# Exchanging rotary halves by DMA for half of layer 0's query heads

## The chip, the cores and the metric

The kernel runs on one core of one Trainium2 chip. The core has a matrix engine (PE; its weight loads are listed apart as PEld), a vector engine (DVE), a scalar engine (ACT), a general engine (POOL), and a queue engine (SP) that here issues the kernel's DMA transfers. The metric is the device time of one execution in microseconds (us), the median of several runs; less is better. A profile is one further execution with a record of each instruction.

## The reference

The program is a decoder of two layers over 64 sequences of 64 tokens, width 256. Each layer does self-attention, cross-attention to a context of the same shape, and a feed-forward part, each behind a layer norm and added to `x`. The change touches layer 0's self-attention only, of which this part matters:

```python
H, HKV, D = (16, 4, 128)
def _rotate_half(x):
    x1, x2 = jnp.split(x, 2, axis=-1)
    return jnp.concatenate([-x2, x1], axis=-1)
qkv = jnp.einsum('bsh,oh->bso', x, w_qkv)
...
q = _layernorm(q, qn_g, qn_b)
k = _layernorm(k, kn_g, kn_b)
cos, sin = _rope_tables(s, D, ROPE_BASE)
q = q * cos + _rotate_half(q) * sin
k = k * cos + _rotate_half(k) * sin
...
scores = jnp.einsum('bhqd,bhkd->bhqk', q, k) / jnp.sqrt(jnp.float32(D))
```

There are 16 query heads of 128 and 4 key and value heads. The rotation adds to each head, times a cosine, the same head with its two halves of 64 exchanged, times a signed sine.

## The kernel before

The 4096 tokens are worked in 16 groups of 256. A group first goes through layer 0 (sections a0, x0 and f0: self-attention, cross-attention, feed-forward), is stored to `mid`, and later goes through layer 1 (a1, x1, f1). Several groups are in work at once, and the preparation of layer 1's weights is mixed into the groups of layer 0.

The order of the work is written by a planner in the kernel itself, before anything runs. Each helper records operations with `s.o(engine, cost, reads, writes, function)`; `s.alt` records an operation that may go to one of several engines. `Sched.plan` then places all operations in one list, by the costs given and by a due time for each one (`LEAD`, `FINE`, `PACE`, `SHIFT`, with penalties such as `PEN` for using DVE for work that may go elsewhere, and `HOLD` for changing how PE is tiled). Each engine gets its instructions in that fixed order, and so does the queue of SP: an instruction that waits holds up all that is listed behind it on its engine. Tiles come from pools with fixed numbers of buffers: `k2` is 2 KB a partition with 67 buffers, `B` is one PSUM bank, with 8.

In self-attention (`l0_attn`) a group is done in two blocks of eight query heads. For each block, `proj2` makes a bank of keys (`k_ps`, two heads by 256 tokens) and four banks of queries (`q_ps`, two heads each, numbered `c2` = 0 to 3), head elements along the partitions. Weights are centred beforehand, so a norm needs only the sum of squares and a factor, which is applied later. `rope_bank` takes such a bank out of PSUM:

- L832, ACT: two copies of 64 partitions each put the halves, exchanged, into the SBUF tile `sw`.
- L833, ACT: the square of `sw` into `sq`, which PE sums up over partitions into `ss` (L857 for keys, L881 for queries).
- L834, DVE: the bank times the cosines `rp0c` (queries) or `rp4c` (keys) into `qu` or `ku`.
- L835, POOL: `sw` times the sines `rp0s` or `rp4s`.
- L837, POOL or DVE: `sw` is added to `qu` or `ku`.

The sums `ss` then pass a chain: ACT (`sss`, L887), a transpose on PE (`ss_t`, L892), a reciprocal root on DVE (`nr_t`, `nr_y`, L606 to L614), then a factor for the keys (`rb`, `rk`, `kf`, L899 to L911). Scores `s_ps` (L933) need `kf` and the four `qu`. After them come the softmax (`sm_mx`, `sm_sm`, `phl`, L625 to L655), a transpose of `phl` by DMA (L578), the product with the values (`po`, L689), its eviction by ACT (L694) and DVE (L696), and the output projection (`acc`). The values lie in `vt` and are also copied, half a tile of 64 partitions each time, to `vx` and back within `vt` (L668 to L670, from SBUF to SBUF, issued by SP).

Cross-attention of layer 0 has scores `xs_ps` (L1033) whose maxima DVE takes (`xmx`, L1040), collected by `mx_ps`, and scores `xt_ps` (L1067) whose exponentials ACT takes (`xpt`, L1074), multiplied with values into `xo_ps` (L1083) and copied to `so` on ACT or DVE. In layer 1 the banks `qk_ps` become `k8` and `q8` on ACT (two halves) or DVE (L1646, L1650).

Of the kernel before, what the change touches and what calls it, by code (L numbers as in the profile page):

```python
# [9 lines left out]
F32 = mybir.dt.float32  # L10
# [10 lines left out]
S = 64  # L21
# [15 lines left out]
HOLD = 965  # L37
# [698 lines left out]
def l0_attn_setup(e, I):  # L736
# [62 lines left out]
    for i, f in ((0, 128.0 ** -0.5), (4, 1.0)):  # L799
        tb = [s.fixed(c.tile([128, S], F32, name=f"rp{i}{n}")) for n in "csb"]  # L800
        tmp = s.T("k1", [128, S], name="rp_tmp")

        def g(rt, cols, cg, sg, bt, b2, i=i, f=f):
            nc.vector.tensor_scalar(cg, rt[:, 0], cols[:, i:i + 1], f, ALU.mult, ALU.mult)
            nc.vector.tensor_scalar(sg, rt[:, 1], cols[:, i + 1:i + 2], f, ALU.mult, ALU.mult)
            nc.vector.tensor_scalar(bt, rt[:, 0], cols[:, i + 2:i + 3], f, ALU.mult, ALU.mult)
            nc.vector.tensor_scalar(b2, rt[:, 1], cols[:, i + 3:i + 4], f, ALU.mult, ALU.mult)
            nc.vector.tensor_tensor(bt, bt, b2, ALU.add)
        s.o("DVE", 700, [rt, cols], tb + [tmp], g)
        w.tab.append(tb)  # L810
    one = c.tile([128, 3, 32], F32, name="onehot")
# [9 lines left out]
def rope_bank(e, ps, tab, dst):  # L821
# [16 lines left out]
    return sq  # L838


def l0_attn(e, xt):
# [5 lines left out]
    for blk in range(2):  # L847
# [24 lines left out]
        for c2 in range(4):  # L872
            ps = s.T("B", [128, 2, GT], name="q_ps")
            proj2(e, w.u[1 + blk], 256 * c2, xT, ps)
            sqs.append(rope_bank(e, ps, w.tab[0], (qu[c2], lambda t: t)))
# [969 lines left out]
def ctx_scale(e, I, nt):  # L1845
# [16 lines left out]
PEN = 247.38  # L1862
NQ = 1
LEAD = {
    ".xt": -7500, "a0.acc": 6500, "a0.bias_ps": -16000, "a0.bm": -112500, "a0.k_ps": -6000, "a0.kf": -4000,
    "a0.ku": -27000, "a0.ln_mv": 86500, "a0.ln_nb": -120000, "a0.ln_rs": 43000, "a0.ln_st": 60500, "a0.nr_v": -2500,
    "a0.nr_y": -92000, "a0.ohl": -35000, "a0.phl": -9500, "a0.po": -500, "a0.pt": 36500, "a0.qu": -2500,
    "a0.rb": 21500, "a0.rk": 2000, "a0.s1": -4500, "a0.s_ps": -27500, "a0.sm_mx": 120000, "a0.sm_sm": -2500,
    "a0.sq": -2000, "a0.ss": 15500, "a0.ss_t": -7000, "a0.sss": 30500, "a0.sw": 38000, "a0.v_ps": -50000,
    "a0.vt": 84000, "a0.vx": 111500, "a0.xT": -26500, "a0.xh": 112500, "a0.xhl": -29000, "a0.xt": -3000,  # L1870
    "a1.ctx1": -38500, "a1.k1": -120000, "a1.k1_ps": -24500, "a1.ksh": 26000, "a1.kst": -32000, "a1.ln_mv": 96000,
    "a1.ln_nb": -55000, "a1.ln_rs": 68500, "a1.ln_st": 120000, "a1.o1_ps": 47500, "a1.oT1": 23000, "a1.pT": -31000,
    "a1.phl": -101000, "a1.q1": 119500, "a1.q1_d": -9500, "a1.q1_ps": -56500, "a1.q1hl": 26500, "a1.q1st": 120000,
    "a1.s1": 120000, "a1.s1_ps": -90500, "a1.sm_f": -3000, "a1.sm_mx": -76000, "a1.sm_sm": 104000, "a1.v1": 90000,
    "a1.vbd": 10500, "a1.xT": 37000, "a1.xh": -8500, "a1.xhl": -6000, "a1.xt": 73500, "f0.-": -112500,
    "f0.f0_ps": -19500, "f0.f0o_ps": -14500, "f0.hT": -69000, "f0.hm": -120000, "f0.hm_ps": 20500, "f0.ln_mv": -4000,
    "f0.ln_nb": 39000, "f0.ln_rs": 42000, "f0.ln_st": 52000, "f0.xT": 78000, "f0.xh": 24000, "f0.xhl": -18000,
    "f0.xt": -11000, "f1.f1ah": 114500, "f1.f1am": -13000, "f1.f1ix": -115500, "f1.f1o": -116500, "f1.f1o_ps": -4500,
    "f1.f1s2": 73500, "f1.f1sx": 81500, "f1.gu": 8500, "f1.gu_ps": -112500, "f1.hq": -53500, "f1.hqT": 93500,
    "f1.ln_mv": 81500, "f1.ln_nb": -116500, "f1.ln_rs": -3000, "f1.ln_st": 31000, "f1.sig": 32000, "f1.xh": -10500,  # L1880
    "f1.xq": -119500, "f1.xqT": 111000, "f1.xt": 30500, "setup.-": 15500, "setup.a1am": 100500, "setup.am_ps": -4000,
    "setup.bo_ps": 70500, "setup.bo_w": -46500, "setup.cen": -72500, "setup.ctx_a": 64000, "setup.ctxa1": 99000,
    "setup.f_t": -94500, "setup.f_w": 23000, "setup.fam": -23500, "setup.fw_ps": 40000, "setup.g_G": -68500,
    "setup.g_ps": -75500, "setup.g_w": -21000, "setup.l0cols": 87500, "setup.l0ek": 7500, "setup.l0eq": -32500,
    "setup.l0w0": -3500, "setup.l0w1": -120000, "setup.l0w2": 67000, "setup.l0w3": 14000, "setup.l0w4": 96000,
    "setup.n_am1": 11500, "setup.n_o": -60000, "setup.n_ps": -116500, "setup.n_v": 120000, "setup.n_w": -28500,
    "setup.nf": 31500, "setup.p2_ar": -85500, "setup.p2_p2": -64500, "setup.rope_t": -34000, "setup.rp_tmp": -49000,
    "setup.sqj": -80000, "setup.w_a1": -25000, "setup.w_a1o": -110500, "setup.w_am1": -59000, "setup.w_f0": -77500,
    "setup.w_hl": -18500, "setup.w_l0kv": 7000, "setup.w_l0o0": -4000, "setup.w_l0o1": -7500, "setup.w_l0q0": -77000,
    "setup.w_l0q1": 26000, "setup.w_n": 47000, "setup.w_x1ki0": -30500, "setup.w_x1ki1": -15500,  # L1890
    "setup.w_x1q0": -64500, "setup.w_x1q1": 14500, "setup.x1wki0": 18500, "setup.x1wki1": 116500,
    "setup.x1wn0": 33500, "setup.x1wn1": 41000, "setup.x1wn2": 77500, "setup.x1wn3": 56000, "setup.x1wq0": 25500,
    "setup.x1wq1": -93500, "setup.xtwo": -62500, "x0.-": -120000, "x0.cT": -11500, "x0.ctx": 9000, "x0.hl": -82000,
    "x0.hl_d": -42500, "x0.ln_mv": -10000, "x0.ln_nb": -71000, "x0.ln_rs": -118000, "x0.ln_st": -103000,
    "x0.mneg": -99500, "x0.mx_ps": -37500, "x0.so": -80000, "x0.xh": 24500, "x0.xmx": -105500, "x0.xo_ps": 3500,
    "x0.xot_ps": 49500, "x0.xpt": 13500, "x0.xrc": -17500, "x0.xs_ps": -16500, "x0.xt": -41000, "x0.xt_ps": 2500,
    "x0.y": -35000, "x0.yo": -82500, "x1.acc": -38000, "x1.cTs": -120000, "x1.chl": 68500, "x1.ctx": -50000,
    "x1.gac": 42000, "x1.gjk": -34000, "x1.gy_ps": 48000, "x1.k8": -29500, "x1.ln_mv": 74500, "x1.ln_nb": -119500,
    "x1.ln_rs": -55000, "x1.ln_st": 87000, "x1.ms": -111500, "x1.phl": 6000, "x1.pt": 64000, "x1.q8": -90000,
    "x1.qk_ps": 17500, "x1.rkL": 103000, "x1.rkb": -88500, "x1.rkb_ps": -49000, "x1.rms": 24500, "x1.s1": 120000,  # L1900
    "x1.s_ps": -120000, "x1.sm_mx": -22000, "x1.sm_sm": -68500, "x1.vn": 117000, "x1.vn_ps": 68000,
    "x1.x1esc": -45000, "x1.xT": 88000, "x1.xh": 116000, "x1.xhl": 117000, "x1.xt": 23500,
}
RESV = 1e+15
TMIN = {"setup.w_a1": 1457, "setup.w_l0kv": -4579, "setup.w_x1q1": 1916, "setup.x1wki1": -18878, "setup.x1wn0": 1785, "setup.x1wn2": -1297, "setup.x1wn3": -2931, "setup.x1wq1": -2255}
FINE = dict(a=[
    (0, 1, -19000), (1, 1, -500), (2, 1, -9000), (3, 1, -13000), (4, 1, 42000), (5, 1, 22500), (6, 1, -11000),
    (7, 1, 10000), (8, 1, 15500), (9, 1, -39000), (10, 1, 1500), (11, 1, -9500), (12, 1, -12500), (13, 1, -15500),
    (14, 1, -5000), (15, 1, 13000), (16, 1, 4000), (17, 1, 9000), (18, 1, -30500), (19, 1, 21500), (20, 1, -45000),
    (21, 3, 500), (24, 1, -34000), (25, 1, 14000), (26, 1, 30500), (27, 1, 5000), (28, 1, 5500), (29, 1, -9000),  # L1910
    (30, 1, 12500), (31, 1, 7500), (32, 1, 21500), (33, 1, 23500), (34, 1, -2000), (35, 1, 44500), (36, 1, -5000),
    (37, 1, 9000), (38, 1, 10500), (39, 1, 6500), (40, 1, 24000), (41, 1, 10000), (42, 1, 6500), (43, 1, 49000),
    (44, 1, -7000), (45, 1, 9500), (46, 1, 10000), (47, 1, 3000), (48, 1, 15500), (49, 1, 10000), (50, 1, 17000),
    (51, 1, -9500), (52, 1, 9000), (53, 1, 10000), (54, 1, 10500), (55, 1, 35500), (56, 1, 3500), (57, 1, 21000),
    (58, 1, 2500), (59, 1, 4000), (60, 1, -500), (61, 1, 1500), (62, 1, -44500), (63, 1, 2000), (64, 1, 21500),
    (65, 1, -37000), (66, 1, -49500), (67, 1, -14000), (68, 1, -5500), (69, 1, -7500), (70, 1, 1000),
    (71, 1, -12500), (72, 1, 38000), (73, 1, -1000), (74, 1, 500), (75, 1, -5000), (76, 1, 4500), (77, 1, 1000),
    (78, 1, 9000), (79, 1, 2500), (80, 1, -4500), (81, 1, 5000), (82, 1, -17000), (83, 1, -12500), (84, 1, 41500),
    (85, 1, -7000), (86, 1, 3500), (87, 1, 7500), (88, 1, 22000), (89, 1, 20000), (90, 1, -8500), (91, 1, -12500),
    (92, 1, -75000), (93, 1, -9000), (94, 1, -12000), (95, 1, -1000), (96, 1, 8000), (97, 1, -5000),  # L1920
    (98, 1, -3000), (99, 1, 4000), (100, 1, -2500), (101, 1, -3000), (102, 1, 12000), (103, 1, 13500),
# [266 lines left out]
```

## Time and profile before

| | us |
|---|---|
| median of 3 runs | 2370.53 |
| lowest and highest | 2370.43, 2375.34 |
| profiled execution, own time | 2375.9 |
| its span, first to last instruction | 2374.1 |

| engine | busy us | share of the span |
|---|---|---|
| PE | 2168.2 | 91% |
| DVE | 1828.7 | 77% |
| POOL | 1691.1 | 71% |
| ACT | 1594.2 | 67% |

The mean clock granted to PE is 0.962 of full speed. DMA moved 220.82 MB. A share of the whole span is a mean over stages: the stores to `mid` end layer 0's groups between 322.1 and 1438.2 us, and the loads of `mid` begin layer 1's between 1154.7 and 2129.2 us, so that a stage with one limit has to be looked at by itself. In the lists below, an idle time in front of an instruction is put down to what ended it; PE is modelled as pipelined, and some of its records are missing.

### The profile page before, as it was taken

What the parts mean: (1) busy time and instruction counts of PE and PEld (TensorE: products, weight loads), DVE (VectorE), ACT (ScalarE), POOL (GpSimd) and SP (SyncE); (2) the same over time, 40 slices, a digit from 0 to 9 for tenths busy, and PEclk for the clock granted to TensorE, in tenths of its full rate; (3) what the DMA queues carried; (4) which work ended last, traced back from release to release, by engine and by line L of the source; (5) the groups of instructions that cost most, each with busy time, mean ns of one, the idle gap of its engine ahead of it and who ended that gap; (6) DMA issues with size and microseconds to landing.
All of it is one profiled execution on the core that took longest, in us unless ns stands there. A gap on an engine that the chain in (4) does not pass through costs nothing. (4 is left out here: it accounts for less than half of the span.)

```text
span 2374.1 us, 69674 instructions
## 1 busy us (share of the span) xinstructions
PE 2168.2 (91%) x28232; PEld 1692.0 (71%) x28232; DVE 1828.7 (77%) x4256; ACT 1594.2 (67%) x3047; POOL 1691.1 (71%) x1793
## 2 busy tenths in 40 slices
PE   6887889988898978999988999999999999999996
PEld 5765556655565645666645788898888988889885
DVE  7577689877878778788887766778877777777766
ACT  7864878777677768788767675666566655656552
POOL 6897898776857677688945664677777667667642
PEclk9997999999899999999989999999999999999997
DMA  7744444342344234244353353444434444343322
GB/s 233 231 118 104 113 110 115 99 110 64 99 112 95 60 62 90 47 114 104 75 157 77 73 108 66 78 86 77 77 79 78 74 81 83 77 79 77 64 33 41
DMA packets 484322, 220.82 MB, mean 93 GB/s; under 512 B 340568, under 2 KB 463384, under 8 KB 484000
## 3 DMA queue, kind: packets, MB, share of 16 engines
q1 hardware_dynamic: 484000, 216.37, 40.1%
q8 instruction: 222, 3.64, 0.6%
q14 instruction: 100, 0.82, 0.1%
HBM read 89.06 MB, written 34.64 MB: 52 GB/s over the span
## 5 line engine op out<-in xcount | busy, mean ns | idle before, releaser
L1541 PE MATMUL vn_ps<-x1wn,cTs 128*64 128x256 f16 x6144 | 357.9, 273 | 0.5 <-ACT q L1282 0.5
L1074 ACT ACTIVATE xpt<-xt_ps,xes 128x512 f32<-128x512 f32 x512 | 316.2, 699 | 61.8 <-PE xt_ps L1067 56.1
L1541 PEld LDWEIGHTS <-cTs 128*64 128x64 f16 x6144 | 327.1, 110 | 17.0 <-issue 15.1
L1040 DVE TENSOR_REDUCE xmx<-xs_ps 128x2 f32<-128x512 f32 x512 | 316.5, 679 | 27.5 <-PE xs_ps L1033 27.0
L626 POOL TENSOR_TENSOR s<-s,sm_mx 128x1024 f32<-128x1024 f32 x96 | 183.6, 1913 | 196.1 <-DVE sm_mx L625 118.3
L1546 ACT ACTIVATE vn<-vn_ps 128x512 f16<-128x512 f32 x256 | 149.2, 593 | 137.8 <-PE vn_ps L1541 136.2
L1548 DVE SCALAR_TENSOR_TENSOR vn<-vn_ps,vn 128x512 f16<-128x512 f32 x256 | 170.7, 680 | 87.2 <-ACT vn L1546 86.7
L655 POOL TENSOR_TENSOR phl<-s,phl 128x512 f16<-128x512 f32 x192 | 221.9, 1166 | 17.7 <-ACT phl L654 13.4
L652 POOL TENSOR_TENSOR s<-s,sm_sm 128x512 f32<-128x512 f32 x192 | 201.5, 1062 | 7.2
L835 POOL TENSOR_TENSOR sw<-sw,rp0s 128x512 f32<-128x512 f32 x128 | 164.8, 1296 | 15.1 <-ACT sq L833 12.9
L654 ACT CAST phl<-s 128x512 f16<-128x512 f32 x192 | 118.4, 620 | 81.5 <-POOL s L652 80.9
L832 ACT COPY sw<-q_ps 64x512 f32<-64x512 f32 x256 | 146.9, 579 | 32.0 <-PE q_ps L432 24.4
L837 POOL TENSOR_TENSOR qu<-qu,sw 128x512 f32<-128x512 f32 x128 | 163.4, 1283 | 2.0
L1650 ACT ACTIVATE k<-qk_ps,x1kb 128x256 f32<-128x256 f32 x240 | 100.6, 471 | 95.1 <-PE qk_ps L432 94.8
L1083 PE MATMUL xo_ps<-xpt,xve 128*32 128x256 f32 x2048 | 150.6, 404 | 7.9 <-ACT xpt L1074 6.1
L569 ACT ACTIVATE xh<-xt,ln_nb,ln_rs 128x256 f32<-128x256 f32 x192 | 107.2, 599 | 61.2 <-POOL ln_nb L566 60.8
L430 PE MATMUL q_ps<-xT,l0w 128*128 128x256 f16 x512 | 140.8, 275 | 2.0 <-ACT mneg L1044 0.8
L430 PE MATMUL acc<-l0w,ohl 128*128 128x256 f16 x512 | 141.2, 276 | 0.5 <-DVE ohl L696 0.4
L432 PE MATMUL q_ps<-xT,l0w 128*128 128x256 f16 x512 | 140.4, 274 | 0.7 <-DVE l0w L541 0.7
L431 PE MATMUL acc<-l0w,ohl 128*128 128x256 f16 x512 | 141.0, 275 | 0.0
L432 PE MATMUL acc<-l0w,ohl 128*128 128x256 f16 x512 | 140.9, 275 | 0.1
L430 PE MATMUL qk_ps<-cTs,x1wki 128*128 128x256 f16 x512 | 140.8, 275 | 0.0
(416 smaller groups left out, 6697.8 us busy)
## 6 DMA issues: line engine op xcount, KB each, us to landing
ovl<-hl_d SPq DMA_DIRECT2D x96, 128.0 KB
vx<-vt SPq DMA_DIRECT2D x64, 128.0 KB
ctx<-in_ctx_dram SPq DMA_DIRECT2D x32, 256.0 KB
hl_d<-hl SPq DMA_DIRECT2D x64, 128.0 KB
wd<-w_hl SPq DMA_DIRECT2D x32, 256.0 KB
q1st<-q_d SPq DMA_DIRECT2D x128, 64.0 KB
xt<-in_x_dram SPq DMA_DIRECT2D x16, 256.0 KB
ctx_a<-in_ctx_dram SPq DMA_DIRECT2D x8, 512.0 KB
```

Of the source, the lines that this page charges most:

```text
L430: nc.tensor.matmul(out, lh, rh, start=(st and i == 0), stop=False, **kw)
L432: nc.tensor.matmul(out, ll, rh, start=False, stop=(i == n - 1), **kw)
L626: s.o("POOL", 1900, [mx], [s1], lambda m, t: nc.gpsimd.tensor_tensor(t, t, bc(m, 2, 64), ALU.subtract))
L652: s.o("POOL", 1030, [sm], [s1.sub(j)], lambda m, t, h=h: nc.gpsimd.tensor_tensor(t[:, h], t[:, h], bc(m[:, h], 2, 64), ALU.mult))
L655: s.alt([("POOL", c_pool(482), lambda t, _, p, h=h: nc.gpsimd.tensor_tensor(pl(p, 1), t[:, h], pl(p, 0), ALU.subtract)), ("DVE", c_dves(51 ...
L835: s.o("POOL", 1225, [sg], [sw], lambda t, w: nc.gpsimd.tensor_tensor(v(w), v(w), bc(t, 1, 8), ALU.mult))
L837: ("POOL", 1225, lambda w, d: nc.gpsimd.tensor_tensor(view(d), view(d), w, ALU.add))], [sw], [dt])
L1040: nc.vector.tensor_reduce(m[:, h, bs % 4, :], p, AX.X, ALU.max))
L1074: nc.scalar.activation(t, p, AF.Exp, scale=a))
L1083: nc.tensor.matmul(o[32 * hh:32 * hh + 32, hs, :], v[:, n, a:a + 32], r[hh][:, n, :], start=(n == 0 and hs == 0), stop=(n == 1), skip_grou ...
L1541: nc.tensor.matmul(r[-1][64 * h:64 * h + 64, p, :], x[:, b // 2, a, k, t], w.part(r, c, 2 * (2 * p + h) + k), start=(n == 0), stop=(n == 5))
L1548: nc.vector.scalar_tensor_tensor(v(l), p, 2.0 ** -15, v(h), ALU.mult, ALU.subtract))
```

## The change

For the query banks with `c2` of 0 and 1 (`SWAPPED = 2`), 64 of the 128 query banks, a new helper `rope_swap` stands in place of `rope_bank`. DVE multiplies the bank in PSUM by the sines, with rows exchanged beforehand in a table `rp0x`, into a tile `swp`. Two DMA transfers of 64 partitions on SP's queue then write the halves of `swp`, exchanged, to `swd`. ACT squares the bank straight from PSUM. DVE multiplies the bank by the cosines, as before, and DVE or POOL adds `swd` to `qu`. Keys, and the queries with `c2` of 2 and 3, keep `rope_bank`. The table `rp0x` is made once by two small transfers. With this go new numbers for the planner, and so a new order of all instructions on all engines.

```diff
-HOLD = 965
+HOLD = 652
...
+    sx = w.sgx = s.fixed(c.tile([128, S], F32, name="rp0x"))
+    for h in range(2):
+        s.o("SP", DMA_NS, [w.tab[0][1]], [sx.sub(h)], lambda a, b, h=h:
+            nc.sync.dma_start(b[64 * h:64 * h + 64], a[64 - 64 * h:128 - 64 * h]))
...
+def rope_swap(e, ps, cg, sgx, dt):
+    nc, s = e.nc, e.s
+    v = lambda t: t.rearrange("p c (b s) -> p (c b) s", s=S)
+    sq, sp, sw = (s.T("k2", [128, 2, GT], name=n) for n in ("sq", "swp", "swd"))
+    s.o("DVE", c_dve(512), [ps, sgx], [sp], lambda p, t, d: nc.vector.tensor_tensor(v(d), v(p), bc(t, 1, 8), ALU.mult))
+    for i in range(2):
+        s.o("SP", DMA_NS + 600, [sp], [sw.sub(i)],
+            lambda p, w, i=i: nc.sync.dma_start(w[64 * i:64 * i + 64], p[64 - 64 * i:128 - 64 * i]))
+    s.o("ACT", c_act(512), [ps], [sq], lambda p, q: nc.scalar.activation(q, p, AF.Square))
+    s.o("DVE", c_dve(512), [ps, cg], [dt], lambda p, t, d: nc.vector.tensor_tensor(v(d), v(p), bc(t, 1, 8), ALU.mult))
+    s.alt([("DVE", c_dves(512), lambda w, d: nc.vector.tensor_tensor(d, d, w, ALU.add)),
+           ("POOL", 1225, lambda w, d: nc.gpsimd.tensor_tensor(d, d, w, ALU.add))], [sw], [dt])
+    return sq
+SWAPPED = 2
...
-            sqs.append(rope_bank(e, ps, w.tab[0], (qu[c2], lambda t: t)))
+            if c2 < SWAPPED:
+                sqs.append(rope_swap(e, ps, w.tab[0][0], w.sgx, qu[c2]))
+            else:
+                sqs.append(rope_bank(e, ps, w.tab[0], (qu[c2], lambda t: t)))
...
-PEN = 247.38
+PEN = 254.99
...
-SPACE = (7285, 2674)
+SPACE = (7304, 2369)
-SHIFT = -31810.49
+SHIFT = 7631.44
-PACE = dict(a=(81129.88, 2.24), b=(66158.31, 2.05))
+PACE = dict(a=(80445.79, 2.17), b=(66336.85, 2.02))
-WINDOW = (5, 6)
+WINDOW = (5, 7)
```

The tables `LEAD` (a lead for each tile's operations), `FINE` (one for each operation of a group) and `TMIN` (earliest times in the setup) also change, nearly every entry of the first two.

## The prediction

> **What bounds the kernel now.** I read the table of stages first. Its columns are busy time in microseconds (us), with the number of instructions behind it, for matmuls (PE), weight loads (PEld), DVE, ACT and POOL; then the granted clock and the DMA share.
>
> ```profile
> core 0: us, PE busy (x) PEld busy (x) DVE busy (x) ACT busy (x) POOL busy (x), PEclk, DMA share, GB/s
> 0.00:150.00 150.00, 120.66 (x1048) 99.53 (x1050) 99.18 (x276) 114.46 (x235) 119.07 (x131) 1.00 0.69 202
> 150.00:1300.00 1150.00, 1007.01 (x11575) 674.87 (x11570) 918.89 (x2156) 844.53 (x1533) 875.34 (x855) 0.94 0.39 97
> 1300.00:2300.00 1000.00, 988.66 (x14868) 873.65 (x14867) 762.05 (x1718) 612.93 (x1243) 671.78 (x777) 1.00 0.40 76
> 2300.00:2374.00 74.00, 51.86 (x753) 43.97 (x751) 48.58 (x110) 22.26 (x38) 24.93 (x31) 0.82 0.22 41
> ```
>
> From 1300 to 2300 us, layer 1, PE is busy 988.7 of 1000 us at full clock: nothing taken from another engine shows there. The changed heads lie in the stage from 150 to 1300. There PE is busy 1007.0 of 1150 us, 143.0 us idle, and its clock is 0.94, which costs about 0.06 x 1007 = 60 us more. Second comes DVE, 918.9 of 1150 or 80%; POOL has 76%, ACT 73%. So PE bounds this stage as well, but loosely: other engines hand their results over late. The waits of PE in this stage say which (engine, line, result, what ended the wait: total us, times, longest):
>
> ```profile
> engine line waited for: us in total, times, longest us
> PE ss L881 <- ACT sq L833: 10.0, 4, 6.8
> PE po L689 <- DMA pt<-phl: 8.2, 11, 1.3
> PE mx_ps L1042 <- DVE xmx L1040: 6.8, 4, 4.7
> ...
> PE xo_ps L1083 <- ACT xpt L1074: 6.1, 9, 1.3
> PE xt_ps L1067 <- ACT xpt L1074: 6.0, 17, 1.8
> PE xt_ps L1067 <- DVE nr_y L614: 5.0, 4, 2.2
> PE s_ps L933 <- POOL kf L911: 4.9, 6, 2.2
> ```
>
> Added by what ended them, all lines of that answer give DVE 56.4, ACT 51.4, DMA 26.5 and POOL 4.9, together 139 of the 143 us. No single wait carries the stage; they are small and spread.
>
> **The parts and their rows.** The groups of instructions by shape give every duration (busy us, then mean ns of one):
>
> ```profile
> L832 ACT COPY sw<-q_ps 64x512 f32<-64x512 f32 x256 | 146.9, 579 | 32.0 <-PE q_ps L432 24.4 <-DVE qu L834 3.3 <-POOL ku L837 0.2
> L833 ACT ACTIVATE sq<-sw 128x512 f32<-128x512 f32 x160 | 100.2, 628 | 3.0 <-POOL qu L837 0.6
> L834 DVE TENSOR_TENSOR qu<-q_ps,rp0c 128x512 f32<-128x512 f32 x128 | 85.5, 680 | 17.4 <-PE q_ps L432 8.5 <-DMA nf_d<-nf 3.9 <-ACT sw L832 3.4
> L835 POOL TENSOR_TENSOR sw<-sw,rp0s 128x512 f32<-128x512 f32 x128 | 164.8, 1296 | 15.1 <-ACT sq L833 12.9 <-DVE xmx L1040 1.5
> ```
>
> There are 128 query banks (16 groups, 2 blocks, 4 banks); the first two of each four change, so 64.
>
> *ACT* loses 2 copies per bank, 128 x 579 ns = 74 us. Its square then reads PSUM; the like row, the 128x512 eviction of L694 at 601 ns, is 27 ns less than 628, so 2 us more. *POOL* loses 64 multiplies by the sines, 64 x 1296 = 83 us; all its additions stay. *DVE* gains 64 multiplies out of PSUM. The nearest row is its own cosine multiply, 680 ns, same shapes and source: 64 x 0.680 = 43.5 us. *PE* does the same matmuls.
>
> The order of instructions also shows that the new plan hands some two-way work to other engines: 15 more layer-1 evictions (k8, q8) on DVE at 691 ns instead of 30 halves on ACT at 471 ns, and 4 copies of so from DVE to ACT at 597 ns. The k8 and q8 lie past 1300 us, where PE is full: I cost them at nothing. If PE waited for each of the 15 it would be 10 us.
>
> Of the L835 group, 112 of 128 lie in the stage, a share of 0.875. There ACT falls by 66 us and gains 2 (844.5 to 780, 68%), POOL falls by 73 (to 803, 70%), DVE rises by 38 and loses 3 (to 954, 83%).
>
> *What that is worth to PE.* Less work helps only through the waits. I scale each engine's waits by its busy time over its free time, an estimate from the stage row: ACT 844.5/305.5 = 2.76 becomes 780/370 = 2.11, a factor 0.76, so 51.4 us of waits lose 12. POOL 3.19 becomes 2.31: 4.9 us lose 1. The wait of ss for sq, 10.0 us, loses a further 3: the square no longer stands behind two copies of its own bank, 1.16 us in each of its 4 waits is 4.6 at most, half of that if only every second wait is of a changed bank, and I take 3 between. DVE goes from 3.98 to 4.87, factor 1.22: its 56.4 us would gain 12. I take half, 6, because the new multiply is not urgent: its result is wanted only by the addition into qu, and qu only by the scores s_ps. There PE and PEld idle 16.0 us for kf and 0.4 us for POOL's qu. So it can lie in DVE's gaps. Both ends stay: 0 and 12.
>
> *The two transfers.* No row shows this copy, but vx<-vt has its shape: 64 partitions, 128 KB, SBUF to SBUF, on the same SP queue; the issue takes 0.57 to 0.59 us (median of L668 and L669). 128 of them are 74 us of SP's time, 65 in the stage. What it costs is landing time:
>
> ```profile
> SPq L670 <- DMA vx<-vt: 26.1, 12, 5.8
> ```
>
> SP waited on average 2.2 us for such a copy to land, and at most 5.8. So a swapped half takes some 2.8 to 6.4 us where two ACT copies and POOL's multiply took 1.16 + 1.30 = 2.5. The extra is off the path as long as qu has the slack named above; qu of the first two banks in each four is also the one made first. If it were on the path, 64 x (2.8 - 2.5) = 19 us would be the low end and 64 x 3.9 = 250 the high end; I take zero, being nearest the row with 0.4 us. The bytes, 128 x 128 KB = 16.8 MB on 220.8 MB, raise the DMA share from 0.39 to about 0.43; by that I add 2 us to the 26.5 us of waits for DMA. The third tile per bank (swp beside swd and sq) takes one more of the 67 buffers for a few us; no wait in the trace is for such a buffer, so 0. The two setup copies of the sines stand among the first 25 issues and are needed after 45 us: 0.
>
> The page "DMA: Bandwidth & Descriptors" of the Trainium skill (section "Anatomy of one DMA") speaks against the change: it puts a fixed cost of about 2.0 us on a DMA however small, most of it the receipt of the last byte. By it the pair would land about 2.3 us after its issue, against 1.16 us for the two ACT copies, and with no slack 64 x 1.1 = 73 us would be lost. Its fit was taken on another issuing path.
>
> *The queue of SP.* The transfers wait for DVE's multiply, and SP works in order, so everything listed behind them waits too: transposes of phl and xh (L578), whose landings already cost PE the 8.2 us above, and the copies of vx and vt. SP stands waiting for POOL's phl alone 65.8 us in the stage, so it has room; I price this at 0 in the sum and as a rival below.
>
> *The clock.* In the stage 143 us of idleness goes with 60 us of slow clock, 0.42 for one. A page of the skill, "TensorE: Matmul & The Clock Gate" (section "What's actually happening"), would allow less: it gives a window of about 3.4 us, and the waits shown are mostly shorter, which by it would make this term nearly zero.
>
> *The sum.* -12 -1 -3 +6 +2 = -8 us; with the clock x 1.42, about -12 us. The profiled execution took 2375.9 us (span 2374.1 plus 1.8 around it): 2364. It lies 5.4 above the median of 2370.5, so the median after should be about 2359.
>
> *What the sum can't hold.* All priorities of the plan are new, so on every engine the order differs throughout. Its bounds come from the windows of this trace: in 200 us PE idles 14.4 (1000 to 1200) to 27.5 us (600 to 800). A stage all like the best would idle 5.75 x 14.4 = 83 us, 60 less than now; all like the worst 158, 15 more.
>
> **The rivals.**
> *Larger gain.* The plan comes near the best windows throughout: half of those 60 us with the clock, -43, about 2328. For it: two of three helpers lose 8%. Against: DVE, owner of the largest waits, gains.
>
> *No change.* DVE takes all back: -16 + 12 + 2 = -2, with the clock -3: about 2367.
>
> *Slower: DVE becomes late.* DVE is at 0.90 from 300 to 400 us and 0.89 from 700 to 800. Two multiplies instead of one hold a PSUM bank 0.68 us longer; of 56 banks in the stage, half awaited by PE gives 19 us. -16 + 12 + 2 + 19 = 17, with the clock 24: about 2394. It decides where DVE passes 0.9 over 100 us.
>
> *Slower: the queue.* Pairs waiting at SP's head delay the transposes; the 26.5 us of DMA waits double: 26.5 - 8 = 18, with the clock 26: 2396.
>
> *That the change doesn't do what it says* is out: the order of instructions shows 64 new multiplies, 128 transfers and 128 fewer copies.
>
> **How the numbers follow.** Small gain 0.46, larger gain 0.16, no change 0.12, DVE late 0.16, queue 0.10. A measurement can tell about 0.2% (4.7 us) from none. Faster is 0.62, within 0.12, slower 0.26. The range, 2326 to 2392, reaches from the larger gain to just below the two slow cases and leaves out about a fifth; small gain alone would be 2345 to 2366.
>
> **What would show it.** Right: in the first 1300 us ACT about 66 and POOL 73 us less busy, DVE about 35 more; sine multiplies near 680 ns; PE's idle time there down by some 8 us, waits for ACT down, for DVE up; layer 1 unchanged at 65 us a group (its 16 loads of xt are issued from 1154.7 to 2129.2 us). Wrong: PE or DVE waiting for swd or qu, SP's waits for swp ahead of transposes, longer waits for PSUM banks, or a fall in idleness that the ACT and POOL lines don't explain, which would be the new order's work.

## The result: slower by 0.8%

The changed kernel takes 2392.28 us (median of 7 runs, 2382.12 to 2397.26), the kernel before, measured beside it, 2373.22 (2369.62 to 2377.25). The ratio is 1.008, with a 95% interval of 1.0057 to 1.0102: 19 us slower, just past the upper end of the range given (2392), where 2359 was forecast, some 12 us faster. A second measurement of the same kernel, told below, gave 2389.96 against 2373.43, a ratio of 1.0070 (1.0052 to 1.0088). The profiled execution took 2396.9 us, its span is 2395.0.

### The profile page after: what moved, and what is told of

Its sections match the earlier page's. It is cut to its first block, busy times and chain, and to the rows that moved or that the text cites. A ratio compares the mean times of both kernels' runs of the same rounds, so it can differ in the third digit from the quotient of the medians.

```text
span 2395.0 us, 69942 instructions
## 1 busy us (share of the span) xinstructions
PE 2155.7 (90%) x28232; PEld 1690.2 (71%) x28232; DVE 1870.3 (78%) x4330; ACT 1520.6 (63%) x2896; POOL 1608.5 (67%) x1727
## 4 chain that ended last, share of the span: by engine, by line
PE 45%; DVE 15%; POOL 15%; DMA 10%; ACT 8%; issue 6%; SPq 1%; POOLq 0%; ACTq 0%; DVEq 0%
PE vn_ps L1569 9%; DVE xmx L1068 4%; PE qk_ps L430 3%; ACT xpt L1102 3%; PE qk_ps L432 3%; PE qk_ps L431 3%; PE acc L1592 3%; PE xo_ps L1111 2%; POOL phl L655 2%; DMA pT<-phl 2%; DMA xT<-xhl 2%; POOL s L652 2%; PE s_ps L961 1%; POOL s L626 1%; PE s_ps L1690 1%
## 5 line engine op out<-in xcount | busy, mean ns | idle before, releaser
L430 PE MATMUL q_ps<-xT,l0w 128*128 128x256 f16 x512 | 140.9, 275 | 8.4 <-ACT nf L1441 3.0
L432 PE MATMUL q_ps<-xT,l0w 128*128 128x256 f16 x512 | 140.7, 275 | 0.0
L431 PE MATMUL q_ps<-xT,l0w 128*128 128x256 f16 x512 | 140.7, 275 | 0.0
L430 PE MATMUL qk_ps<-xT,x1wq 128*128 128x256 f16 x512 | 139.7, 273 | 0.0
L432 PE MATMUL qk_ps<-xT,x1wq 128*128 128x256 f16 x512 | 139.6, 273 | 0.0
L431 PE MATMUL qk_ps<-xT,x1wq 128*128 128x256 f16 x512 | 139.6, 273 | 0.0
```

Of the source, the lines that this page charges most:

```text
L430: nc.tensor.matmul(out, lh, rh, start=(st and i == 0), stop=False, **kw)
L431: nc.tensor.matmul(out, lh, rl, start=False, stop=False, **kw)
L432: nc.tensor.matmul(out, ll, rh, start=False, stop=(i == n - 1), **kw)
```

## The profile after

The table of stages, with the columns as before:

```profile
core 0: us, PE busy (x) PEld busy (x) DVE busy (x) ACT busy (x) POOL busy (x), PEclk, DMA share, GB/s
0.00:150.00 150.00, 111.13 (x879) 91.18 (x880) 95.39 (x255) 96.52 (x203) 97.03 (x111) 0.91 0.75 201
150.00:1300.00 1150.00, 992.56 (x11506) 674.38 (x11508) 943.50 (x2203) 771.93 (x1411) 798.60 (x794) 0.95 0.46 110
1300.00:2300.00 1000.00, 980.54 (x14793) 862.16 (x14784) 769.54 (x1733) 621.11 (x1229) 684.75 (x787) 1.00 0.41 77
```

ACT and POOL are relieved as computed (844.5 to 771.9 and 875.3 to 798.6 us), and DVE has its extra. Yet PE does less in both first stages: 111.1 us against 120.7 in the first 150, and 992.6 against 1007.0 in the next 1150 (111.6 and 999.4 in a second profile of the changed kernel). What has risen besides DVE is the DMA share, from 0.69 to 0.75 and from 0.39 to 0.46. The granted clock of the first 150 us fell from 1.00 to 0.91, but it is 0.94 there in the first kernel of the experiments below, which loses nothing. Layer 1 goes on at the old pace: its 16 loads of `xt` are issued from 1170.0 to 2148.3 us, 65 us apart as before, only 15 to 19 us later. Most of the loss is made before it.

The groups by shape give the parts (busy us, mean ns):

```profile
L852 DVE TENSOR_TENSOR swp<-q_ps,rp0x 128x512 f32<-128x512 f32 x64 | 43.7, 682 | 8.1 <-PE q_ps L432 5.3 <-ACT sq L856 2.2 <-POOL qu L842 0.5
L856 ACT ACTIVATE sq<-q_ps 128x512 f32<-128x512 f32 x64 | 38.1, 596 | 12.0 <-PE q_ps L432 11.2
L837 ACT COPY sw<-q_ps 64x512 f32<-64x512 f32 x128 | 74.1, 580 | 47.4 <-PE q_ps L432 41.4 <-POOL qu L859 1.9 <-DVE qu L839 1.4
```

The sine multiply takes 682 ns (680 forecast), the square out of PSUM 596 (601), and half of the copies are gone. The waits of PE from 150 to 1300 us, the largest and those that answer to the ones shown before:

```profile
engine line waited for: us in total, times, longest us
PE acc L432 <- DVE ohl L696: 12.4, 6, 9.9
PE ss L909 <- ACT sq L838: 11.1, 3, 9.6
PE xot_ps L1123 <- ACT so L1116: 10.6, 12, 1.7
PE f_ps L430 <- DMA xT<-xhl: 7.6, 7, 2.6
...
PE po L689 <- DMA pt<-phl: 6.2, 6, 2.0
...
PE ss L882 <- ACT sq L856: 3.1, 2, 2.6
```

Summed by what ended them they are DVE 59.4, ACT 57.1, DMA 30.2 and POOL 7.9 (before: 56.4, 51.4, 26.5 and 4.9). In the second profile they are 59.9, 50.9, 29.0 and 7.6. None has clearly fallen, ACT's not either, although ACT does 73 us less. Two more lines are about the transfers themselves: SP's wait for DVE in the same stage (total, times, longest), and what POOL's addition waited for over the whole span (from the view of the tile `swd`: total, times).

```profile
SPq L855 <- DVE swp L852: 61.3, 18, 10.4
```

```profile
its engine sat idle before it (us, times) until:
  DMA swd<-swp: 13.2, 9
```

Read alone, these two lines suggest that the loss is SP standing at the head of its queue, or the addition waiting for the landing. The experiments were made to tell.

## The experiments

Five accounts were open. *Queue*: SP stands at a pair until DVE has multiplied, and what is listed behind it goes late. *Landing*: the addition waits for the pair. *Load*: the bytes hold the 16 DMA engines, whoever waits for them. *DVE*: 64 more multiplies. *Order*: the new plan is worse by itself. Each kernel below was timed against the kernel before on the same chip; ratios are to it, with 95% intervals. The code cuts are shortened: `...` and plain words stand for code that is left out.

### Four first cuts: transfers, multiplies, order

No transfers, in the changed kernel's order (the addition takes `swp` as it is):

```diff
-    sq, sp, sw = three tiles
+    sq, sp, sw = three tiles; sw.same = sp
-            lambda p, w, i=i: nc.sync.dma_start(w[64 * i:64 * i + 64], p[64 - 64 * i:128 - 64 * i]))
+            lambda p, w: None)
```

> The changed kernel with its order of instructions kept on every engine, but the 128 transfers are not issued: the addition takes swp itself, so the halves stay unexchanged (that part of the computation is left out). If the loss of 19 us comes from the transfers (their landing, or their place in SP's queue), the time goes back to about 2373 us. If it comes from the new order or from DVE's extra multiply, it stays at 2385 us or more.

Measured: 2370.94 us, ratio 0.9976 (0.9959 to 0.9994). The whole loss hangs on the transfers. What is left of the change, relieved ACT and POOL against a fuller DVE in the new order, is a gain of 3 to 6 us.

No sine multiplies, transfers kept (they exchange the product with the cosines, which DVE makes at the sines' place):

```diff
-    s.o("DVE", ..., [ps, sgx], [sp], sines)
-    s.o("DVE", ..., [ps, cg], [dt], cosines)
+    s.o("DVE", ..., [ps, sgx], [sp], cosines)      # sp is dt
+    s.o("DVE", ..., [ps, cg], [dt], nothing)
```

> The changed kernel with its order kept, but DVE's 64 multiplies by the sines are left out (the cosine multiply is done in their place, and the transfers exchange its result). If DVE's 43.5 us of extra work cause the loss, the time goes back to about 2373 us or below. If the order or the transfers cause it, it stays at 2383 us or more.

Measured: 2382.06 us, ratio 1.0029 (1.0011 to 1.0048). That is between the times of the two accounts. Against 1.007 to 1.008 for the changed kernel the 64 multiplies are worth 10 to 12 us, a smaller part than the transfers.

The old work in the new order (ACT's copies stand where the square stands, POOL's multiply where the addition stands; no transfers, no sine multiplies on DVE):

```diff
+    def square(p, q):
+        for i in range(2):
+            nc.scalar.copy(sp[64 * i:64 * i + 64], p[64 - 64 * i:128 - 64 * i])
+        nc.scalar.activation(q, sp, AF.Square)
+    def add(w, d):
+        nc.gpsimd.tensor_tensor(v(w), v(w), bc(sines, 1, 8), ALU.mult)
+        nc.gpsimd.tensor_tensor(d, d, w, ALU.add)
```

> The changed kernel's order on all engines, with the old work put back into it: two ACT copies in front of the square, POOL's multiply in front of its addition, no sine multiply on DVE and no transfers for any bank. If the swap itself costs the time (transfers or DVE), this returns to 2370 to 2378 us. If the new order costs it, this stays at 2390 us or goes above, to 2410, since ACT and POOL have about 75 and 83 us more to do than the order was made for.

Measured: 2440.70 us, ratio 1.0267 (1.0225 to 1.0309). That is above what either account gave. The planned order fits its own work: with the copies and POOL's multiplies where the plan had put none it is 70 us slower than the kernel without transfers. So this run says nothing on whether the order is good, only that work can't be put into a foreign order for free.

The new work in the old order (multiply at the place of the first copy, transfers at the square's place, wherever a buffer was free; the trace has 124 transfers of 128):

```diff
     def copy(p, w, i):
-        nc.scalar.copy(w[64 * i:64 * i + 64], p[64 - 64 * i:128 - 64 * i])
+        if i == 0: nc.vector.tensor_tensor(v(w), v(p), bc(e.l0.x, 1, 8), ALU.mult)
     def square(p, q):
-        nc.scalar.activation(q, p, AF.Square)
+        nc.scalar.activation(q, ps.real, AF.Square)
+        for i in range(2):
+            nc.sync.dma_start(swd[0][64 * i:64 * i + 64], p[64 - 64 * i:128 - 64 * i])
```

> The kernel before with its order on all engines, with the swap put into it for 61 of the 64 banks (where a buffer is free): DVE's sine multiply at the place of the ACT copies, the transfers at the place of the square, POOL's multiply left away. If the new order costs the time and the swap itself is neutral or helps, this gives 2355 to 2376 us. If the swap itself costs it, this gives 2385 us or more.

Measured: 2395.37 us, ratio 1.0085 (1.0058 to 1.0113), the loss of the changed kernel. So the loss does not need the new order. That the order has no part in it is not shown by this run: its new work stands at places that were not planned for it, and the run before shows what that can cost.

### Which part of a transfer: landing, queue, load

Everything issued as in the change, but the addition takes `swp`, so nobody waits for a landing:

```diff
-    ... nc.gpsimd.tensor_tensor(d, d, w, ALU.add)
+    ... nc.gpsimd.tensor_tensor(d, d, sp.real, ALU.add)
```

> Left out of the computation: the rotary halves are not exchanged (the add takes the sine products as DVE wrote them). All 128 transfers are still issued from SP, in their places, and still wait there for the sine multiply; but no instruction waits for them to land, except a later user of the same buffer. Three prices are apart here. Landing (the add stands until both transfers have landed, and the square sums, the logits and PE behind it): the loss of 21 us goes, 2371 to 2376 us. Head of the queue (SP stands at a pair until DVE has multiplied, and the transfers queued behind it go late): the loss stays, 2385 to 2395. Load (16.8 MB more on the DMA engines and 128 more issues in SP's queue): the loss stays too, 2385 to 2395.

Measured: 2386.66 us, ratio 1.0065 (1.0044 to 1.0086). The loss stays; landing is not it.

In addition, the source is a weight tile that is long written, so SP hardly stands at the pairs either (25 us in the first 1300, against 108 in the changed kernel):

```diff
-            lambda p, w, i=i: nc.sync.dma_start(w[64 * i:64 * i + 64], p[64 - 64 * i:128 - 64 * i]))
+            lambda p, w, i=i: nc.sync.dma_start(w[64 * i:64 * i + 64], e.l0.u[0].tiles[0].real[64 - 64 * i:128 - 64 * i]))
```

> Left out of the computation: the exchange, as in the run before; in addition the 128 transfers read a part of layer 0's weights of the same bytes (2 KB in each of 64 partitions) instead of the sine products. So SP does not stand at them for DVE, and nobody waits for them to land; the issues and the load on the DMA engines are left. Head of the queue: 2371 to 2376 us here while the run before stays at 2385 or more. Landing: both at 2371 to 2376. Load: both at 2385 to 2395.

Measured: 2388.16 us, ratio 1.0073 (1.0053 to 1.0093). The loss stays; the queue's head is not it. A third way to take the pairs out of SP's queue, whole and with the exchange, is to issue them from ACT:

```diff
-            lambda p, w, i=i: nc.sync.dma_start(...)
+            lambda p, w, i=i: nc.scalar.dma_start(...)
```

> The whole computation; the 128 transfers are issued from ACT's queue instead of SP's, at their places in the same order. Head of the queue: SP no longer stands for DVE, and most of the 21 us comes back, unless ACT's own wait for DVE and its issuing take it: 2373 to 2385 us. Landing: the add waits as long as before, 2388 to 2396. If an issue takes ACT as long as it takes SP (0.58 us, 128 of them, 74 us, what the removed copies took): ACT is as busy as before the change, 2390 to 2405.

Measured: 2396.55 us, ratio 1.0109 (1.0088 to 1.0130). It is no better, by its ratio rather worse. In its profile the pairs have a queue of their own (packets, MB, share of the 16 DMA engines):

```profile
q10 hardware_dynamic: 10240, 16.79, 2.9%
```

An issue takes ACT a median of 494 ns, 128 of them 63 us, most of what the removed copies took, so this run alone doesn't tell the load from ACT's extra work. That the loss stays agrees with the page "DMA: Bandwidth & Descriptors" of the Trainium skill (section "Issuing engines are not separate DMA queues"), which says that transfers from all issuing engines end on the same 16 DMA engines.

Last of this set, the changed kernel itself again:

> The changed kernel itself, beside the three that follow and again beside the kernel before. Load theory (the 128 transfers cost by the time they hold the DMA engines and by standing in one queue with the rest, whoever waits for them): 2388 to 2392 us, 16 to 19 us over the kernel before, as the two runs in which nobody waited for a landing (15 and 17 us over it). Landing theory (the add's wait has a price of its own on top): 2392 to 2396 us, 20 us or more over it.

Measured: 2389.96 us, ratio 1.0070 (1.0052 to 1.0088). With and without the addition's wait the ratios are 1.0070, 1.0065 and 1.0073: the landing has no price outside these intervals, some 5 us.

### Bytes or issues

As with the ready source, but 64 bytes a partition and not 2048:

```diff
-            w[64 * i:64 * i + 64], ...real[64 - 64 * i:128 - 64 * i]
+            w[64 * i:64 * i + 64, 0:32], ...real[64 - 64 * i:128 - 64 * i, 0:32]
```

> Left out of the computation: the exchange. As in the run with the ready source (128 transfers in their places, from a source that is long written, nobody waits for them), but each moves 64 bytes in each of 64 partitions instead of 2048: as many issues and as many rows, a thirty-second of the bytes. If the price is bytes (the time for which the DMA engines are held): 2371 to 2375 us, as without the transfers. If it is the issue, 0.58 us of SP's queue for each: 2386 to 2390, as with the full ones.

Measured: 2370.20 us, ratio 0.9987 (0.9975 to 1.0000). 128 issues, at a median of 587 ns of SP's time each, cost nothing that shows in this order; the bytes are the price. Half of the bytes (`0:512` in the same place):

> Left out of the computation: the exchange. As the runs with the ready source (128 transfers, nobody waits), with 1024 of the 2048 bytes in each partition. A price that follows the bytes: half way between 2370 and 2388, 2377 to 2382. A price that begins only where the DMA engines are full: 2370 to 2375.

Measured: 2379.46 us, ratio 1.0018 (1.0005 to 1.0032). It lies between none (0.9987) and all (1.0073), a little under the middle and within its interval of it.

The decisive run leaves the kernel before as it is, with its own order and work, and adds only the bytes:

```diff
     def square(p, q):
         nc.scalar.activation(q, p, AF.Square)
+        if sw.swap:
+            d = s.pools["k2"].tile([128, 4 * GT], F16, tag="k2", name="swd")
+            for i in range(2):
+                nc.sync.dma_start(d[64 * i:64 * i + 64], e.l0.u[0].tiles[0].real[64 - 64 * i:128 - 64 * i])
```

> The kernel before, whole, in its own order, with its ACT copies and POOL multiplies; added are the pairs of transfers of 128 KB each for the banks of the first two query chunks (some 62 of 64, where a buffer is free), from a part of the weights that is long written into a buffer that nobody reads. Bytes alone: 14 to 20 us over the kernel before (2386 to 2393). If the bytes cost only together with the change's order or with its fuller DVE: within 5 us of the kernel before.

Measured: 2392.81 us beside 2374.57, ratio 1.0071 (1.0051 to 1.0091). The bytes alone, 124 transfers that nobody needs, cost 17 us, about as much as the whole change loses. Of the engines' waits only one, of 0.4 us, is for one of them, and SP stands at them for 8 us in all. Their 124 issues, a median of 588 ns each, are in the 17 us too; that issues are free was measured in the changed kernel's order only. The stage of this kernel:

```profile
150.00:1300.00 1150.00, 1001.03 (x11481) 668.72 (x11479) 910.13 (x2115) 837.58 (x1518) 864.91 (x843) 0.93 0.44 107
```

ACT, POOL and DVE have their old work, the DMA share is 0.44 and not 0.39, and PE is behind. The engines themselves are not slowed by much: the copies of the halves take 580 ns (579 before), the cosine multiplies 683 (680). Nor is the clock the cause: its mean over all runs is 0.963, and 0.964 for the kernel before beside it, which is worth some 2 us of PE's 2168 (an estimate). Where the loss may enter is seen in the waits for other transfers in the first 1300 us, here of this kernel (DVE, ACT, PE):

```profile
DVE fam L1726 <- DMA f_w<-in_w_dn_dram: 11.3, 1, 11.3
```

```profile
ACT hl L1012 <- DMA ctx<-in_ctx_dram: 20.3, 5, 14.6
```

```profile
PE f_ps L449 <- DMA xT<-xhl: 9.5, 6, 2.4
```

and the same of the kernel before:

```profile
DVE fam L1699 <- DMA f_w<-in_w_dn_dram: 7.5, 1, 7.5
```

```profile
ACT hl L985 <- DMA ctx<-in_ctx_dram: 13.9, 4, 11.7
```

```profile
PE f_ps L430 <- DMA xT<-xhl: 6.4, 4, 2.4
```

A weight load, the context and a transpose are each waited for longer, 3.8 + 6.4 + 3.1 = 13.3 us more on three engines. Only the last is a wait of PE for a DMA; the others can reach PE as a late DVE or ACT, which would explain why the sum of PE's DMA waits hardly rose (28.0 us in the stage against 26.5). These are three of the lines that rose most; others fell, and all waits of PE, DVE, ACT and POOL for a DMA in the first 1300 us went from 87.7 to 98.6, 11 us more. In the changed kernel it is DVE that waits longer for DMA, 21.7 and 22.9 us in two profiles, against 10.3 without transfers and 13.5 with 64 bytes a partition, while the context is waited for less than before (5.0 us). So the bytes are shown to cost the time; the way by which they do, other transfers that land late, is an inference from single profiles.

### Early or late

No transfers in the first three groups of 16 (`if s.grp < 3: sw.same = sp`, and no issue there):

> Left out of the computation: the exchange in layer 0's first three groups of 16, whose 24 transfers are not issued (the add takes the sine products unexchanged); the other 104 transfers are as in the changed kernel. Startup theory (against the run without any transfer, the changed kernel falls back by 10 us between 92 and 119 us from its start, where the weights are still being loaded, and by some 1.3 us in each later group): 24 transfers of 128 are worth about half of the loss, 2379 to 2383 us. Even theory (each transfer costs the same wherever it is): 24 / 128 of 21 us = 4 us, 2387 to 2390.

Measured: 2378.62 us, ratio 1.0041 (1.0026 to 1.0056). And the transfers of these three groups alone:

> Left out of the computation: the exchange in layer 0's groups 3 to 15, whose 104 transfers are not issued; the 24 of the first three groups are, and waited for. Startup theory: these 24, of which about 10 lie in the 90 us in which the DMA engines are full with the weights (share 0.98 between 60 and 90 us without them), cost 8 to 12 us: 2379 to 2384. Even theory: 24 / 128 of 21 us = 4: 2373 to 2376.

Measured: 2375.40 us, ratio 1.0015 (1.0002 to 1.0027). Counted from the two kernels without these bytes (0.9976 and 0.9987), the 24 early transfers cost 7 to 9 us, 0.3 to 0.4 each, and the 104 others 13 to 15 us, 0.12 to 0.15 each; together they make up the whole. By these ratios an early one costs two to three times as much as a later one, not four or five times, and the later ones are not free. But each ratio is uncertain by 3 to 4 us, and the two times disagree on the accounts: 2375.40 lies in the range of the even price, 2378.62 just under that of the startup. An equal price for all is not ruled out by them. These kernels have the same instructions in the same order, so their start times can be compared one by one. By how many us DVE's instructions start later than in the kernel without transfers (one profile each, to about 0.5 us):

```
DVE instruction at (us)     64   125   186   668   970  1091  2304
changed kernel             0.8  10.7  12.0  17.7  25.9  29.8  26.2
first three groups only    0.8  10.5  11.2  12.8  13.0  13.5   9.4
all but the first three    0.4   0.1  -4.8  -0.4   8.7   9.8   9.1
64 bytes a partition      -0.2   2.5   1.2   2.4   1.3   2.2   1.6
```

Some 10 us are lost at once between 64 and 125 us, while the weights still come in (12 in the second profile of the changed kernel). In the kernel before with the bytes added it is not so: against the kernel before, DVE starts 1 us later at 125 us, 4 at 186 and 17 at 2304, although 18 of its transfers are issued in the first 150 us and 16 in the changed kernel. So the early loss seems to belong to this order. The windows of the kernel without transfers, then of the changed one, suggest a reason:

```profile
60.00:90.00 30.00, 29.07 (x261) 24.77 (x262) 23.09 (x61) 24.50 (x52) 20.20 (x21) 1.00 0.98 283
```

```profile
60.00:90.00 30.00, 26.52 (x183) 21.93 (x183) 19.72 (x51) 21.37 (x46) 19.78 (x21) 0.94 0.97 275
```

Here the DMA engines are full already (0.98, 283 GB/s), so the bytes of a transfer come in place of others: PE starts 183 matmuls and not 261 (203 in the second profile, 243 with 64 bytes a partition). Ten of the 128 transfers are issued by 91.1 us; 10 x 131 KB at 283 GB/s is 4.6 us, and 6.7 us by the 0.67 us each that is worked out at the end: half to two thirds of what is lost there. The rest is not explained.

### The exchange without a transfer

Every version with these bytes loses, so DVE itself did the exchange: two multiplies of 64 partitions, reading one half in PSUM and writing the other half's partitions.

```diff
+        for i in range(2):
+            a, b = slice(64 - 64 * i, 128 - 64 * i), slice(64 * i, 64 * i + 64)
+            nc.vector.tensor_tensor(v(d)[b], v(p)[a], bc(t[a], 1, 8), ALU.mult)
```

> The whole computation, with no transfer: DVE's sine multiply is split in two of 64 partitions, each reading one half of the bank in PSUM and writing the other half's partitions, so that the exchange is done in the multiply; ACT and POOL stay relieved as in the change. 64 more DVE instructions of some 0.68 us: 44 us more of DVE. The removal of as many cost 10 us less in an earlier run without them, so if DVE's time is worth the same upward: 2371 + 10 = 2381 us (2376 to 2390). If DVE, at 0.82 of the stage, becomes the bound: 2395 or more.

Measured: 2389.41 us, ratio 1.0078 (1.0059 to 1.0096).

```profile
L863 DVE TENSOR_TENSOR swp<-q_ps,rp0x 64x512 f32<-64x512 f32 x128 | 88.1, 688 | 6.7 <-PE q_ps L438 3.6 <-ACT sq L867 0.5
```

```profile
150.00:1300.00 1150.00, 994.98 (x11484) 674.19 (x11483) 980.78 (x2249) 771.72 (x1409) 795.76 (x793) 0.95 0.39 96
```

With the DMA share back at 0.39, 64 multiplies more put DVE at 980.8 of 1150 us, 85%, and cost 19 to 24 us over the kernels without these bytes, about twice what the first 64 cost. PE's waits for DVE in the stage are 66.8 us. Half of it, in the order of the kernel before:

> The whole computation, in the order of the kernel before, with no transfer: for the first query chunk of each four (32 banks, not 64) DVE does the exchange in two sine multiplies of 64 partitions, and ACT's two copies and POOL's multiply go; the rest is as before. DVE gets 64 x 0.68 = 44 us more, ACT 37 and POOL 40 less. A price in proportion: half of the 16 us of the full exchange, 2379 to 2383. A price that grows with DVE's load: 2370 to 2376; under 2370 it beats both kernels.

Measured: 2397.43 us, ratio 1.0094 (1.0074 to 1.0115), worse than either theory said. PE's waits for DVE are 80.8 us there. The multiplies stand where that plan had ACT's copies, ahead of work that the plan wanted from DVE next; that this is the reason is not shown. No kernel tried beat the one before by more than 3 to 6 us, and those that did (no transfers, 64 bytes) leave the exchange out.

## Why the prediction was wrong

**The step that failed is the price of the transfers.** Their bytes were put in at +2 us (with the clock 3), by scaling the 26.5 us in which PE waits for DMA with the DMA share. The bytes cost 17 us in the kernel before, and 20 to 25 in the changed one (1.0070 to 1.0080 against 0.9976 and 0.9987). Together with the gain that was left, 3 to 6 us, this gives the 17 to 19 us of loss. Three things were wrong in the scaling. PE's own waits for DMA were the wrong base: they are 26.5 us before, 30.2 and 29.0 after and 28.0 with the bytes alone, so the price does not show in them; that DVE, ACT and POOL wait for loads and hand it on under their own names is the likely way. The 16.8 MB were set against the 220.8 of the whole span, but all of them lie in the first 1160 us: from 150 to 1300 the traffic rose by 13%, from 97 to 110 GB/s, and the share to 0.46, not 0.43. And the stage row of the prediction showed a share of 0.69 for the first 150 us, where no price was set at all.

**Landing and queue were priced at 0, and rightly.** POOL's addition waited 9 times, SP stood 61.3 us, and neither moved the end. The 19 to 250 us for landing on the path did not come about. Nor did the fixed cost of about 2.0 us a transfer, which the page "DMA: Bandwidth & Descriptors" of the Trainium skill (section "Anatomy of one DMA") gives, show in the time: with the addition's wait the ratio is 1.0070, without it 1.0065. The reason given for the queue was no reason: that SP stands 65.8 us for `phl` is not room, since a standing SP holds up what is behind it. The third tile, also put at 0, shows in one place: an ACT copy into another tile of `k2` (`nf`), which does not read a pair, waited 5.6 us for one to land; with 64 bytes a partition that wait is 4.6 us, and no time is lost.

**The queue rival gave 2396, near the result, by the wrong mechanism.** It wanted PE's waits for DMA doubled by pairs at SP's head. They rose from 26.5 to 30.2, and the loss stayed when SP hardly had to wait. That its number came close is luck.

**The gain was overestimated.** Busy times and durations were right to about 1%, but the terms -12 -1 -3 +6, with the clock -14, came to -3 (64 bytes a partition) to -6 us (no transfers), both in the new order. PE's waits for ACT did not fall with ACT's load: they are 51.3 and 53.0 us in these two kernels against 51.4 before, where a factor of 0.76 was used. A wait for a result that is late because its source is late need not scale with how busy its engine is. The wait of `ss` for `sq`, from which 3 us were to go, is 11.1 + 3.1 us after. DVE's term, 6 with ends at 0 and 12, and with the clock 8.5, is 10 to 12 by the run without the sine multiplies; it grows to 19 to 24 for the next 64, which the rival of a late DVE had in kind, though DVE reached at most 0.88 in a window of 100 us and not the 0.9 that it named. Its 2394 is near the result by luck too: with the same multiplies and no transfers the kernel is faster than the one before.

**The clock term** was not tested by itself. Over runs beside each other the mean granted clock is 0.964 for the kernel before and for the changed one, 0.969 with 64 bytes a partition and 0.968 with the exchange on DVE, which is as slow as the changed kernel: the time does not follow the clock alone.

**The new order** was bounded at -60 to +15. The old order loses the same with the new work (1.0085), and the kernel before loses about as much with the bytes alone, so nothing calls for a part of the order. No run isolates it.

## What to carry to other kernels

Price a transfer by what it does to the other transfers, not only by who waits for it: look at the DMA share by stage, and at the waits of every engine for a DMA, since a load that lands late can show up on PE as a late DVE or ACT. Set the bytes against the traffic of the stage in which they lie, not of the whole span. A transfer that nobody waits for is still not free. Where a suspect can be added to the kernel before with nothing else changed, that run is a cleaner test than one that takes it out of the kernel after, whose order was planned around it.

## What the runs showed of the hardware

The main DMA queue (packets, MB, share of the 16 engines' span), in the kernel before and with the bytes added to it:

```profile
q1 hardware_dynamic: 484000, 216.37, 40.1%
```

```profile
q1 hardware_dynamic: 493920, 232.63, 43.3%
```

The 124 added transfers of 128 KB raise its time from 40.1% of 2374.1 us to 43.3% of 2391.2 us, 83 us, or 0.67 us of all 16 DMA engines for each; about a fifth of this, 0.14 us each, comes out at the end, although the engines are idle for more than half of the stage. The fit in the page "DMA: Bandwidth & Descriptors" of the Trainium skill (section "Anatomy of one DMA"), taken on another issuing path, would give, as an estimate, 131072 / 436e3 = 0.30 us for the moving part of one; here it is twice that, measured as shares of packet time.

A DVE multiply of 64 partitions and 512 elements takes 688 ns, as long as one of 128 partitions (682), so halving the partitions saves nothing here.
